# A Mamba-2 block in fp32: B times C and the state's output as one matmul group per row half of the TensorE array, on a PSUM ring of five banks

## The chip, the cores and the metric

One core of a Trainium2 chip runs the kernel. The metric is the device time of one execution in microseconds; less is better. All matrices are fp32. TensorE (PE in the profile) writes its products into PSUM, which has eight banks of 128 partitions by 2 KB; VectorE (DVE) and ScalarE (ACT) read them from there; GpSimd (POOL) works on SBUF alone; DMAs are issued from the queue of SyncE (SP).

## The reference

The block works on an input of 4 batches by 512 tokens by 512 channels. Six modulation vectors per batch come from a small matmul of `silu(c)`. Then:

```python
h = layernorm(x) * (1 + ca) + sa
x = x + ga * mamba2(h)                 # ga: at least 0.25 in size, sign kept
h = layernorm(x) * (1 + cb) + sb
x = x + gb * (h @ binarized(weight).T + bias)
```

and inside `mamba2`, with 64 heads of 16 channels, 8 groups of B and C with a state of 64, and chunks of 128 tokens:

```python
xBC, z, A = split(h @ in_proj_w.T)             # 2048, 1024 and 64 columns
xBC = silu(causal_conv_of_4_taps(xBC) + bias)  # then split into x, B, C
dt  = softplus(A);  dA = -dt
Lm  = exp(segsum(dA))                          # 128 x 128 decays for each head and chunk
Y_diag = (C B^T * Lm) X                        # within a chunk
Y_off  = C state * exp(cumsum(dA))             # from the chunks before
y   = (Y_diag + Y_off + D * x / dt) * silu(z + z_bias)
out = y @ out_proj_w.T
```

The state is carried from chunk to chunk of a batch (four chunks). `X` is the convolved x itself, as `x / dt * dt`.

## The kernel before

**Staging.** The 2048 tokens are cut into eight halves `h` of 256 tokens (two to a batch), each of two chunks `c` of 128 tokens. The 8 groups are taken in four pairs `gp`. A unit is `(h, c, gp)`, so there are 64 units, eight to a half. A unit has two groups, `r` = 0 and 1, which lie on partitions 0 to 63 and 64 to 127 of the tiles of B, C and the state; each has eight heads.

**Front of a half.** `f_norm` and `f_hT` make the normalized, transposed, modulated input. `f_dt` makes everything from `dt`: `pa` is the projection (L306); VectorE's softplus series follows (L309 to L322, one dependent step after another, with Abs and Exp on ACT at L310 and L311), ending in `ndt`; then `pe` (L330, L331) gives the decays to the chunk's end, `pc` (L344) the running sums, which go to DRAM (`sums_d`, `e_d`) to be read back broadcast over partitions; `pn` and `pr` (L353, L359) are transposes of small tiles. `f_B`, `f_C`, `f_x` are pairs of 128 columns of the input projection (L367 in `proj`) with the convolution: ACT's first tap at L379, VectorE's three taps at L383, tanh at L387, and the last product at L391. `f_C` writes C into `cd`, a tile with zeros in it: group `r` sits on its own 64 partitions and in its own 256 columns, block-diagonally, so that one matmul over all 128 partitions gives both groups. `f_Bt` and `f_xt` transpose B and x (`to_tokens`, L399). `f_z` projects the gate (L451 to L457).

**A unit** has three stages. `stage0` loads the running sums into two `decay` tiles and `e` by DMA. `stage1` multiplies B by C (`pg`, L509; 256 columns through `cd`), masks the result on VectorE (`gm`, L511), takes 16 exponentials on ACT (L516) and multiplies them by `gm` on VectorE (L519, twice). `stage2` forms the state's output (L543, again 256 columns through `cd`; not in a batch's first chunk) and 16 strip matmuls of 32 output columns each (L549), four of which lie side by side in the array; VectorE combines them (`yt`, L557 and L558), POOL finishes (L559, L562); then the new state's part `pst` (L574, two matmuls of 64 columns) is added by VectorE (L584, or copied at L577).

**Tail.** `tail1`, `tail2`, `tail3` do the output projection `po` (L606), the second norm, its transposes `ph` (L621) and the last projection `pf` (L634) for each chunk.

**Order.** The loop at the end calls these functions step by step from the table `FRONT`; step `s` works on unit `s` in `stage2`, on `s + 1` in `stage1` and on `s + 2` in `stage0`. The framework's scheduler then orders the instructions of each engine at build time by priority (the order of the calls) and by its own estimate of when they are ready, and adds the semaphores. Each engine takes its queue in that order. Tiles of one pool and tag share that tag's buffers in turn. PSUM accesses to one bank of one tile are kept in order, whichever part of it they touch.

**PSUM.** Four banks are a ring with the tag "mm" (projections, `po`, `ph`, `pf`), two are a ring "tr" (`pa`, `pe`, `pc`, `pn`, `pr`, `pt`, `pst`, `pm`), one holds `pg`, one `py`.

Of the kernel before, what the change touches and what calls it, by code (L numbers as in the profile page):

```python
# [1 line left out]

# [36 lines left out]
def adaln_mamba_block(  # L39
# [71 lines left out]

    cds = []
    for i in range(3):
        cd = keep.tile([P, 2, 2, T], F32, name=f"cd{i}")
        nc.gpsimd.memset(cd, 0.0)
        cds.append(cd)

    NE = 4
    decays = []
    for i in range(NE):  # L120
        et = keep.tile([P, HPG, CH], F32, name=f"decay{i}")
        nc.gpsimd.memset(et[CH // 2 :, :, 0 : CH // 2], 0.0)
        decays.append(et)


# [57 lines left out]
    def mod_cols(t6, slot):  # L183

        pg = mod_row(t6)
        row = wk.tile([B, DM], F32, tag="h2", name=f"row{t6}")
        nc.vector.tensor_scalar(row, pg, 1.0 if t6 in (1, 4) else 0.0, None, ALU.add)
        pm = ps.tile([P, NK, B], F32, tag="tr", bufs=2, name=f"pm{t6}")
# [15 lines left out]
    def gates_out():  # L204

        grow = wk.tile([B, 3, DM], F32, tag="gates", name="grow", bufs=1)
        brow = wk.tile([B, DM], F32, tag="th", name="brow", bufs=1)
# [88 lines left out]
    def f_dt(h):  # L296
# [5 lines left out]

        pa = ps.tile([P, W], F32, tag="tr", bufs=2, name=f"pa_{h}")
        for c in range(2):
# [23 lines left out]

        pe = ps.tile([P, 2, W], F32, tag="tr", bufs=2, name=f"pe_{h}")
        mm(pe[:, 0, :], after, ndt, start=True, stop=True)  # L330
# [10 lines left out]

        pc = ps.tile([NH, 2, 2, CH], F32, tag="tr", bufs=2, name=f"pc_{h}")
        for c in range(2):
# [6 lines left out]
        nc.sync.dma_start(e_d[h], es)  # L350
        pn = ps.tile([P, W], F32, tag="tr", bufs=2, name=f"pn_{h}")
        for c in range(2):
# [3 lines left out]

        pr = ps.tile([NH, 2, CH], F32, tag="tr", bufs=2, name=f"pr_{h}")
        for c in range(2):
# [10 lines left out]
    def conv_pair(h, t0, name, dst=None):  # L369

        u = wk.tile([P, 2, T], F32, tag="u", name=f"u_{name}_{h}", bufs=2)
# [11 lines left out]
        th = wk.tile([P, 2, T], F32, tag="th", name=f"th_{name}_{h}", bufs=1)  # L386
        nc.scalar.activation(th, u, AF.Tanh)  # L387
        if dst is None:
            dst = [(u, slice(0, P))]
        for d, r in dst:  # L390
            nc.vector.scalar_tensor_tensor(d, th[r], 1.0, u[r], ALU.add, ALU.mult)  # L391
        return u

    def to_tokens(src, name):

        pt = ps.tile([P, 2, 2, P], F32, tag="tr", bufs=2, name=f"pt_{name}")
        for c in range(2):
            for j in range(2):
                nc.tensor.transpose(pt[:, c, j, :], src[:, j, c * CH : (c + 1) * CH], ident)  # L399
        return pt  # L400

    def f_B(h, q):
        t = wk.tile([P, 2, T], F32, tag="B", name=f"B_{h}_{q}", bufs=3)
        conv_pair(h, DI // P + 2 * q, f"B{q}", [(t, slice(0, P))])
# [19 lines left out]
    def f_xt(h, j):  # L424
        xc = H[h].pop("xc")
        pt = to_tokens(xc, f"xt_{h}_{j}")
        xp = xpads[(4 * h + j) % NXP]
        nc.scalar.copy(
            xp.rearrange("p c (i q e) -> p (c i) q e", q=4, e=HD)[:, :, 0:4:3, :],
            pt.rearrange("p c j (i q e) -> p (c j i) q e", q=2, e=HD),  # L430
        )
        H[h]["xt"][j] = xp

        rr = wk.tile([P, 2, T], F32, tag="rr", name=f"rr_{h}_{j}", bufs=1)
        for r in range(2):
            lo = (2 * j + r) * HPG
            nc.sync.dma_start(
                rr[:, r, :],
                r_d[h, lo : lo + HPG].rearrange("h c s -> h (c s)").unsqueeze(1).to_broadcast([HPG, HD, T]),
            )  # L440
        xs = wk.tile([P, 2, T], F32, tag="xs", name=f"xs_{h}_{j}", bufs=4)
        nc.gpsimd.tensor_tensor(xs, xc, rr, ALU.mult)  # L442
        H[h]["xs"][j] = xs

    def f_z(h, j):
        pm = ps.tile([P, 2, T], F32, tag="mm", name=f"pp_z{j}_{h}")
        for q in range(2):
            proj(pm[:, q, :], h, NCONV + (2 * j + q) * P, KS - 1)
        u = wk.tile([P, 2, T], F32, tag="u", name=f"uz_{h}_{j}", bufs=2)
# [4 lines left out]
        th = wk.tile([P, 2, T], F32, tag="th", name=f"thz_{h}_{j}", bufs=1)  # L454
        nc.scalar.activation(th, u, AF.Tanh)
# [40 lines left out]

    def c_pair(h, c, gp):
        return H[h]["C"][gp // 2][:, gp % 2, :, c * CH : (c + 1) * CH]

    def stage1(h, c, gp):  # L500
# [6 lines left out]
        ets, e = U0.pop((h, c, gp))  # L507
        pg = ps.tile([P, 2, CH], F32, tag="g", name=f"pg_{n}", bufs=1)
        mm(pg, H[h]["B"][gp // 2][:, gp % 2, c * CH : (c + 1) * CH], c_pair(h, c, gp), start=True, stop=True)  # L509
        gm = wk.tile([P, 2, CH], F32, tag="gm", name=f"gm_{n}", bufs=3)  # L510
        nc.vector.tensor_mul(gm, pg, bc_mid(upto, 2))  # L511
        hd0 = c * NH + gp * HPP
# [11 lines left out]
    def stage2(h, c, gp):  # L524
# [15 lines left out]

        py = ps.tile([P, 2, 2, CH], F32, tag="y", name=f"py_{n}", bufs=1)
        if k > 0:
            mm(py[:, 1], states[b, k][:, gp, :], c_pair(h, c, gp), start=True, stop=True)  # L543

        for r in range(2):
            for q in range(2):
                for j in range(HPG // 2):
                    i = 2 * j + q
                    mm(py[32 * j : 32 * j + 32, 0, r, :], xp[:, r * 2 * P + 32 * i : r * 2 * P + 32 * i + 32],  # L549
                       ets[r][:, i, :], start=(q == 0), stop=(q == 1))  # L550

# [4 lines left out]
        if k > 0:  # L556
            nc.vector.tensor_mul(t, py[:, 1], e)  # L557
            nc.vector.tensor_add(t, py[:, 0], t)  # L558
            nc.gpsimd.tensor_add(t, t, xs)  # L559
        else:  # L560
            nc.vector.tensor_add(t, py[:, 0], xs)  # L561
        nc.gpsimd.tensor_mul(zg, t, zg)  # L562

        if k < HPB * 2 - 1:
# [111 lines left out]
    for step in range(-1, max(steps) + 1):  # L676
        ahead = step + 1 < len(units)

        late = step < 0 or step % NU == NU - 1
# [12 lines left out]

# [41 lines left out]
```

## Time and profile before

| | |
|---|---|
| median of three runs | 830.69 us (828.16 to 830.78) |
| profiled execution | 828.1 us; span from first to last instruction 826.4 us |
| granted TensorE clock, mean | 0.98 |
| busy: PE, weight loads, DVE, ACT, POOL | 773.7, 531.7, 647.4, 529.2, 258.2 us |
| DMA | 99.26 MB, mean 120 GB/s |

An fp32 matmul appears as two instructions of type MATMUL. In groups of instructions, a row gives the line, the engine, the operation, the tiles (written <- read), the shape, the count, busy time and mean nanoseconds of one, and idle time before it with what ended that. For PE, 128*32 is the part of the array in use, rows by columns; a matmul's shown duration includes its way through the array, so the distance between starts is what one costs in a stream. In the order of time, a row gives the start, the length, the engine and the group, and in brackets the idle time before it with its releaser. In the slices each digit is a tenth of busy time in a fortieth of the span.

### The profile page before, as it was taken

To read this page: it belongs to the slowest core of one execution; us is meant where nothing else is said; L and a number is where in the kernel's file an instruction comes from. 1 tells how busy PE (TensorE), PEld (TensorE's weight loads), DVE (VectorE), ACT (ScalarE), POOL (GpSimd) and SP (SyncE) were. 2 spreads that over 40 slices of the span, in tenths; PEclk is the share of its full clock that TensorE was granted. 3 is DMA by queue.
4 is the path that set the end of the run, shared out by engine and by line. 5 is a ranking of instruction groups with operands and counts; after the bars stand their busy time and mean duration, and the time that the engine had idled before them with its cause. 6 is when DMAs were issued, how large, how long until landed. Compare 5 with 4: busy or idle time off the path is not lost. (4 is left out here: it accounts for less than half of the span.)

```text
span 826.4 us, 14794 instructions
## 1 busy us (share of the span) xinstructions
PE 773.7 (94%) x5008; PEld 531.7 (64%) x5008; DVE 647.4 (78%) x1249; ACT 529.2 (64%) x1510; POOL 258.2 (31%) x293
## 2 busy tenths in 40 slices
PE   5979889999999999999999999999999999999875
PEld 0853657767667767667667767667667766667431
DVE  3688779995899669995899669996899768995742
ACT  0455485677667778577767678476758687676640
POOL 5020312353223412353223412253213521353431
PEclk9979999999999999999999999999999999999986
DMA  8856542525344372425444272344434382343620
GB/s 297 324 136 199 148 103 68 136 62 137 94 116 127 87 180 68 129 70 128 103 112 133 74 190 68 104 94 104 128 101 113 91 204 52 113 103 90 147 58 13
DMA packets 120139, 99.26 MB, mean 120 GB/s; under 512 B 73976, under 2 KB 98552, under 8 KB 120064
## 3 DMA queue, kind: packets, MB, share of 16 engines
q1 hardware_dynamic: 120064, 98.32, 44.9%
q8 instruction: 40, 0.66, 0.4%
q14 instruction: 35, 0.29, 0.1%
HBM read 92.50 MB, written 5.79 MB: 119 GB/s over the span
## 5 line engine op out<-in xcount | busy, mean ns | idle before, releaser
L516 ACT ACTIVATE decay<-decay,st 128x128 f32<-128x128 f32 x1024 | 313.8, 390 | 39.5 <-DMA decay<-sums_d 39.0
L519 DVE SCALAR_TENSOR_TENSOR decay<-decay,gm 128x1024 f32<-128x1024 f32 x128 | 168.4, 1322 | 11.4 <-ACT decay L516 10.6
L367 PE MATMUL pp_x<-hT,win 128*128 128x259 f32 x512 | 124.5, 393 | 3.4 <-DVE u_B L383 3.4
L606 PE MATMUL po<-wout,z 128*128 128x512 f32 x256 | 122.0, 615 | 5.3 <-POOL z L562 5.3
L367 PE MATMUL pp_z<-hT,win 128*128 128x256 f32 x512 | 115.1, 379 | 0.0
L367 PEld LDWEIGHTS pp_x<-hT,win 128*128 128x128 f32 x512 | 95.6, 193 | 23.0 <-issue 7.7
L367 PEld LDWEIGHTS pp_z<-hT,win 128*128 128x128 f32 x512 | 95.4, 189 | 15.7 <-issue 3.3
L549 PE MATMUL py<-decay,xpad 128*32 128x128 f32 x2048 | 81.8, 280 | 6.6 <-DVE decay L519 5.4
L383 DVE SCALAR_TENSOR_TENSOR u_x<-pp_x,cw,u_x 128x256 f32<-128x256 f32 x192 | 81.8, 476 | 2.2 <-ACT u_x L379 1.7
L442 POOL TENSOR_TENSOR xs<-u_x,rr 128x512 f32<-128x512 f32 x32 | 47.2, 1474 | 112.7 <-DVE u_x L391 68.1
L606 PEld LDWEIGHTS po<-wout,z 128*128 128x128 f32 x256 | 47.2, 194 | 51.6 <-issue 44.1
L549 PEld LDWEIGHTS py<-decay,xpad 128*32 128x32 f32 x2048 | 54.1, 111 | 36.0 <-issue 23.8
L569 POOL TENSOR_TENSOR xd<-xpad,ed 128x256 f32<-128x256 f32 x48 | 35.2, 732 | 131.4 <-PE pst L574 101.8
L562 POOL TENSOR_TENSOR z<-yt,z 128x256 f32<-128x256 f32 x64 | 66.7, 1042 | 30.4 <-DVE yt L561 18.9
L559 POOL TENSOR_TENSOR yt<-yt,xs 128x256 f32<-128x256 f32 x48 | 38.9, 811 | 111.1 <-DVE yt L558 110.9
L634 PE MATMUL pf<-bwT,h 128*128 128x512 f32 x128 | 63.5, 636 | 6.6 <-DVE u_x L383 5.8
L367 PE MATMUL pp_B<-hT,win 128*128 128x259 f32 x256 | 60.6, 382 | 0.0
L367 PE MATMUL pp_C<-hT,win 128*128 128x259 f32 x256 | 58.9, 381 | 0.0
L623 ACT ACTIVATE h<-ph,modT 128x128 f32<-128x128 f32 x64 | 24.5, 456 | 48.7 <-PE ph L621 48.7
L451 ACT ACTIVATE uz<-pp_z,zb 128x256 f32<-128x256 f32 x64 | 26.9, 466 | 43.7 <-PE pp_z L367 41.7
L367 PEld LDWEIGHTS pp_B<-hT,win 128*128 128x128 f32 x256 | 47.5, 190 | 11.2 <-issue 4.3
L367 PEld LDWEIGHTS pp_C<-hT,win 128*128 128x128 f32 x256 | 48.4, 190 | 7.4
(129 smaller groups left out, 1083.3 us busy)
## 6 DMA issues: line engine op xcount, KB each, us to landing
decay<-sums_d SPq DMA_DIRECT2D x128, 256.0 KB
decay<-sums_d SPq DMA_DIRECT2D x128, 128.0 KB
rr<-r_d SPq DMA_DIRECT2D x64, 128.0 KB
wm<-in_w_mod SPq DMA_DIRECT2D x24, 256.0 KB
e<-e_d SPq DMA_DIRECT2D x96, 64.0 KB
x<-in_x SPq DMA_DIRECT2D x16, 256.0 KB
win<-in_w_inT SPq DMA_DIRECT2D x4, 1024.0 KB
xr<-in_x SPq DMA_DIRECT2D x16, 256.0 KB
```

What stands on the lines that cost most here:

```text
L367: mm(pm, win[:, k, col : col + P], H[h]["hT"][:, k, lo:], start=(k == 0), stop=(k == NK - 1))
L383: nc.vector.scalar_tensor_tensor(u[:, j, :], pm[:, k : k + T], cw[:, t, k : k + 1], u[:, j, :], ALU.mult, ALU.add)
L442: nc.gpsimd.tensor_tensor(xs, xc, rr, ALU.mult)
L451: nc.scalar.activation(u[:, q, :], pm[:, q, :], AF.Identity, bias=zb[:, 2 * j + q : 2 * j + q + 1], scale=0.5)
L516: nc.scalar.activation(ets[r][:, i, :], ets[r][:, i, :], AF.Exp, bias=H[h]["st"][:, hd : hd + 1])
L519: nc.vector.scalar_tensor_tensor(ets[r], ets[r], 1.0, bc_mid(gm[:, r, :], HPG), ALU.min, ALU.mult)
L549: mm(py[32 * j : 32 * j + 32, 0, r, :], xp[:, r * 2 * P + 32 * i : r * 2 * P + 32 * i + 32], ets[r][:, i, :], start=(q == 0), stop=(q == 1))
L559: nc.gpsimd.tensor_add(t, t, xs)
L562: nc.gpsimd.tensor_mul(zg, t, zg)
L569: nc.gpsimd.tensor_tensor(xd, xg, by_head(H[h]["ed"][:, hd0 : hd0 + HPP]), ALU.mult)
L606: mm(po, H[h]["z"][g // 2][:, g % 2, c * CH : (c + 1) * CH], wout[:, g, :], start=(g == 0), stop=(g == NKI - 1))
L634: mm(pf, h2[:, k, :], bwT[:, k, :], start=(k == 0), stop=(k == NK - 1))
```

## The change

B times C and the state's output are no longer single matmuls against the block-diagonal `cd`. Each becomes two matmuls of 64 rows and 128 columns, one per row half of the array, whose results lie in two PSUM banks, one per row half (`gy`). `cd` and its zero fills are gone; `f_C` writes an ordinary tile with one VectorE instruction. The state's output of unit `s` and B times C of unit `s + 2` form one group, `glued`: its instructions are queued behind its first at a raised priority, ahead of the strips of unit `s`, which form a glued group of their own. `stage1` of unit `s + 2` now follows `stage0` of the same unit, for every step.

PSUM is laid out anew: the ring "mm" has five banks and takes over `pm`, `pe` and `pt`; `gy` holds two banks (slots 0 and 1 for the products, slots 2 and 3, as `pdt`, for `pa`, `pc`, `pn`, `pr` of `f_dt`); one bank, `pyst`, holds `py` and two slots of `pst` in turn. In SBUF `u` has three buffers instead of two, `th` and `rr` two instead of one. The number of lines grows: `pa` is at L309, `pe` at L333, `pf` at L650, the glued matmuls are at L496 (the first of a group) and L499 (the others).

```diff
-    ps = ctx.enter_context(tc.tile_pool(name="ps", bufs=4, space=PSUM))
+    ps = ctx.enter_context(tc.tile_pool(name="ps", bufs=5, space=PSUM))
...
-    cds = []
-    for i in range(3):
-        cd = keep.tile([P, 2, 2, T], F32, name=f"cd{i}")
-        nc.gpsimd.memset(cd, 0.0)
-        cds.append(cd)
...
+    bgy = ctx.enter_context(tc.tile_pool(name="bgy", bufs=1, space=PSUM))
+    gy = bgy.tile([P, 2, 4, CH], F32, name="gy")
+    pdt = gy[:, :, 2:4, :].rearrange("p b q s -> p b (q s)")
+
+    pyst = bgy.tile([P, 4, CH], F32, name="pyst")
...
-        pa = ps.tile([P, W], F32, tag="tr", bufs=2, name=f"pa_{h}")
+        pa = pdt[:, 0, 0:W]
...
-        pe = ps.tile([P, 2, W], F32, tag="tr", bufs=2, name=f"pe_{h}")
+        pe = ps.tile([P, 2, W], F32, tag="mm", name=f"pe_{h}")
...
-        pc = ps.tile([NH, 2, 2, CH], F32, tag="tr", bufs=2, name=f"pc_{h}")
+        pc = pdt[0:NH].rearrange("p c (q s) -> p c q s", q=2)
...
-        cd = cds[(2 * h + q) % 3]
-        conv_pair(
-            h, (DI + NG * NS) // P + 2 * q, f"C{q}",
-            [(cd[r * NS : (r + 1) * NS, :, r, :], slice(r * NS, (r + 1) * NS)) for r in range(2)],
-        )
-        H[h]["C"][q] = cd
+        t = wk.tile([P, 2, T], F32, tag="C", name=f"C_{h}_{q}", bufs=3)
+        conv_pair(h, (DI + NG * NS) // P + 2 * q, f"C{q}", t)
+        H[h]["C"][q] = t
...
+    def glued(products):
+        first = products[0]()
+        with tc.issue_after(first.ins), tc.high_priority(offset=1000):
+            for product in products[1:]:
+                product()
+
+    def by_rows(slot, h, c, gp, stationary):
+        return [
+            partial(
+                mm, gy[:, r, slot, :], stationary[part],
+                H[h]["C"][gp // 2][part, gp % 2, c * CH : (c + 1) * CH], start=True, stop=True,
+            )
+            for r, part in enumerate((slice(0, NS), slice(NS, P)))
+        ]
+
+    def state_out(h, c, gp):
+        k = (h % HPB) * 2 + c
+        return by_rows(1, h, c, gp, states[h // HPB, k][:, gp, :]) if k > 0 else []
+
+    def b_times_c(h, c, gp):
+        return by_rows(0, h, c, gp, H[h]["B"][gp // 2][:, gp % 2, c * CH : (c + 1) * CH])
...
-        pg = ps.tile([P, 2, CH], F32, tag="g", name=f"pg_{n}", bufs=1)
-        mm(pg, H[h]["B"][gp // 2][:, gp % 2, c * CH : (c + 1) * CH], c_pair(h, c, gp), start=True, stop=True)
...
-        py = ps.tile([P, 2, 2, CH], F32, tag="y", name=f"py_{n}", bufs=1)
-        if k > 0:
-            mm(py[:, 1], states[b, k][:, gp, :], c_pair(h, c, gp), start=True, stop=True)
+        py = pyst[:, 0:2, :]
...
-            pst = ps.tile([P, P], F32, tag="tr", bufs=2, name=f"pst_{n}")
+            pst = pyst[:, 2 + (c * NP + gp) % 2, :]
...
-        if ahead and not late:
-            stage1(*units[step + 1])
         for f, args in steps.get(step, []):
             f(*args)
-        if step < 0:
-            stage0(*units[0])
-        if 0 <= step < len(units):
-            stage2(*units[step])
-        if ahead and late:
-            stage1(*units[step + 1])
-        if step + 2 < len(units):
-            stage0(*units[step + 2])
+        new = units[step + 2 : step + 3] if step >= 0 else units[0:2]
+        if step < 0:
+            for unit in new:
+                glued(b_times_c(*unit))
+                stage0(*unit)
+                stage1(*unit)
+        elif step < len(units):
+            products = state_out(*units[step])
+            for unit in new:
+                products += b_times_c(*unit)
+            if products:
+                glued(products)
+            stage2(*units[step])
+            for unit in new:
+                stage0(*unit)
+                stage1(*unit)
```

More of the change, by code (lines that the diff above doesn't have):

```diff
@@ L1 @@
 from contextlib import ExitStack
+from functools import partial
 import numpy as np
@@ L187, in mod_cols @@
         nc.vector.tensor_scalar(row, pg, 1.0 if t6 in (1, 4) else 0.0, None, ALU.add)
-        pm = ps.tile([P, NK, B], F32, tag="tr", bufs=2, name=f"pm{t6}")
+        pm = ps.tile([P, NK, B], F32, tag="mm", name=f"pm{t6}")
         for dt in range(NK):
@@ L206, in gates_out @@
         grow = wk.tile([B, 3, DM], F32, tag="gates", name="grow", bufs=1)
-        brow = wk.tile([B, DM], F32, tag="th", name="brow", bufs=1)
+        brow = wk.tile([B, DM], F32, tag="th", name="brow")
         nc.sync.dma_start(brow, ffn_b.partition_broadcast(B))
@@ L350, in f_dt @@
         nc.sync.dma_start(e_d[h], es)
-        pn = ps.tile([P, W], F32, tag="tr", bufs=2, name=f"pn_{h}")
+        pn = pdt[:, 0, 0:W]
         for c in range(2):
@@ L355, in f_dt @@
         nc.vector.tensor_scalar(st, pn, -1.0, None, ALU.mult)
-        pr = ps.tile([NH, 2, CH], F32, tag="tr", bufs=2, name=f"pr_{h}")
+        pr = pdt[0:NH, 1, :].rearrange("p (c s) -> p c s", c=2)
         for c in range(2):
@@ L369, in conv_pair @@
     def conv_pair(h, t0, name, dst=None):
-        u = wk.tile([P, 2, T], F32, tag="u", name=f"u_{name}_{h}", bufs=2)
+        u = wk.tile([P, 2, T], F32, tag="u", name=f"u_{name}_{h}", bufs=3)
         for j in range(2):
@@ L385, in conv_pair @@
                 )
-        th = wk.tile([P, 2, T], F32, tag="th", name=f"th_{name}_{h}", bufs=1)
+        th = wk.tile([P, 2, T], F32, tag="th", name=f"th_{name}_{h}")
         nc.scalar.activation(th, u, AF.Tanh)
[L388 to L391, printed above, removed]
+        nc.vector.scalar_tensor_tensor(u if dst is None else dst, th, 1.0, u, ALU.add, ALU.mult)
         return u
     def to_tokens(src, name):
-        pt = ps.tile([P, 2, 2, P], F32, tag="tr", bufs=2, name=f"pt_{name}")
+        pt = ps.tile([P, 2, 2, P], F32, tag="mm", name=f"pt_{name}")
         for c in range(2):
@@ L403, in f_B @@
         t = wk.tile([P, 2, T], F32, tag="B", name=f"B_{h}_{q}", bufs=3)
-        conv_pair(h, DI // P + 2 * q, f"B{q}", [(t, slice(0, P))])
+        conv_pair(h, DI // P + 2 * q, f"B{q}", t)
         H[h]["B"][q] = t
     def f_C(h, q):
-        cd = cds[(2 * h + q) % 3]
-        conv_pair(
-            h, (DI + NG * NS) // P + 2 * q, f"C{q}",
-            [(cd[r * NS : (r + 1) * NS, :, r, :], slice(r * NS, (r + 1) * NS)) for r in range(2)],
-        )
-        H[h]["C"][q] = cd
+        t = wk.tile([P, 2, T], F32, tag="C", name=f"C_{h}_{q}", bufs=3)
+        conv_pair(h, (DI + NG * NS) // P + 2 * q, f"C{q}", t)
+        H[h]["C"][q] = t
     def f_Bt(h, q):
@@ L432, in f_xt @@
         H[h]["xt"][j] = xp
-        rr = wk.tile([P, 2, T], F32, tag="rr", name=f"rr_{h}_{j}", bufs=1)
+        rr = wk.tile([P, 2, T], F32, tag="rr", name=f"rr_{h}_{j}")
         for r in range(2):
@@ L448, in f_z @@
             proj(pm[:, q, :], h, NCONV + (2 * j + q) * P, KS - 1)
-        u = wk.tile([P, 2, T], F32, tag="u", name=f"uz_{h}_{j}", bufs=2)
+        u = wk.tile([P, 2, T], F32, tag="u", name=f"uz_{h}_{j}", bufs=3)
         for q in range(2):
@@ L453, in f_z @@
             )
-        th = wk.tile([P, 2, T], F32, tag="th", name=f"thz_{h}_{j}", bufs=1)
+        th = wk.tile([P, 2, T], F32, tag="th", name=f"thz_{h}_{j}")
         nc.scalar.activation(th, u, AF.Tanh)
@@ L495, in stage0 @@
         U0[h, c, gp] = (ets, e)
-    def c_pair(h, c, gp):
-        return H[h]["C"][gp // 2][:, gp % 2, :, c * CH : (c + 1) * CH]
+    def glued(products):
[16 more added lines that the diff above has]
+        return by_rows(0, h, c, gp, H[h]["B"][gp // 2][:, gp % 2, c * CH : (c + 1) * CH])
     def stage1(h, c, gp):
@@ L507, in stage1 @@
         ets, e = U0.pop((h, c, gp))
-        pg = ps.tile([P, 2, CH], F32, tag="g", name=f"pg_{n}", bufs=1)
-        mm(pg, H[h]["B"][gp // 2][:, gp % 2, c * CH : (c + 1) * CH], c_pair(h, c, gp), start=True, stop=True)
         gm = wk.tile([P, 2, CH], F32, tag="gm", name=f"gm_{n}", bufs=3)
-        nc.vector.tensor_mul(gm, pg, bc_mid(upto, 2))
+        nc.vector.tensor_mul(gm, gy[:, :, 0, :], bc_mid(upto, 2))
         hd0 = c * NH + gp * HPP
@@ L539, in by_head @@
             return v.rearrange("p (j q) -> p j q", q=2).unsqueeze(3).to_broadcast([P, HPG, 2, HD])
-        py = ps.tile([P, 2, 2, CH], F32, tag="y", name=f"py_{n}", bufs=1)
-        if k > 0:
[L543 to L550, printed above, removed]
+        py = pyst[:, 0:2, :]
+        glued([
+            partial(
+                mm, py[32 * j : 32 * j + 32, r, :],
+                xp[:, r * 2 * P + 32 * (2 * j + q) : r * 2 * P + 32 * (2 * j + q) + 32],
+                ets[r][:, 2 * j + q, :], start=(q == 0), stop=(q == 1),
+            )
+            for r in range(2) for q in range(2) for j in range(HPG // 2)
+        ])
         cs = slice(c * CH, (c + 1) * CH)
@@ L556, in stage2 @@
         if k > 0:
-            nc.vector.tensor_mul(t, py[:, 1], e)
-            nc.vector.tensor_add(t, py[:, 0], t)
+            nc.vector.tensor_mul(t, gy[:, :, 1, :], e)
+            nc.vector.tensor_add(t, py, t)
             nc.gpsimd.tensor_add(t, t, xs)
         else:
-            nc.vector.tensor_add(t, py[:, 0], xs)
+            nc.vector.tensor_add(t, py, xs)
         nc.gpsimd.tensor_mul(zg, t, zg)
@@ L676, in adaln_mamba_block @@
     for step in range(-1, max(steps) + 1):
-        ahead = step + 1 < len(units)
-        late = step < 0 or step % NU == NU - 1
-        if ahead and not late:
-            stage1(*units[step + 1])
         for f, args in steps.get(step, []):
             f(*args)
+        new = units[step + 2 : step + 3] if step >= 0 else units[0:2]
         if step < 0:
-            stage0(*units[0])
-        if 0 <= step < len(units):
+            for unit in new:
[8 more added lines that the diff above has]
+                glued(products)
             stage2(*units[step])
-        if ahead and late:
-            stage1(*units[step + 1])
-        if step + 2 < len(units):
-            stage0(*units[step + 2])
+            for unit in new:
+                stage0(*unit)
+                stage1(*unit)
 _OUT = ((B, L, DM), np.float32)
```

## The prediction

> **What bounds the kernel now.** I read the page's totals and slices first, then the stretches, then the order of time around the spots that the change touches.
>
> ```profile
> PE 773.7 (94%) x5008; PEld 531.7 (64%) x5008; DVE 647.4 (78%) x1249; ACT 529.2 (64%) x1510; POOL 258.2 (31%) x293
> PE   5979889999999999999999999999999999999875
> DVE  3688779995899669995899669996899768995742
> PEclk9979999999999999999999999999999999999986
> ```
> TensorE is busy nearly all the time between the ramp and the tail, at full clock. The view of stretches says it sharper: of the 100 us from 125 to 225, PE is busy for 99.45, DVE for 83.81, ACT for 67.79. So in the middle a microsecond of TensorE work, or of TensorE waiting, is a microsecond of the kernel.
>
> The order of time on TensorE, once around a half's `f_dt` (from `pa` to `pe`):
>
> ```profile
> 301.33 1.22 PE L306 MATMUL pa<-win,hT 128*128 128x64 f32 x10
> 302.39 5.37 PE L606 MATMUL po<-wout,z 128*128 128x512 f32 x12
> 307.60 3.67 PE L367 MATMUL pp_B<-hT,win 128*128 128x259 f32 x16
> 311.11 3.67 PE L367 MATMUL pp_C<-hT,win 128*128 128x259 f32 x16
> 314.61 0.59 PE L543 MATMUL py<-cd,S 128*128 128x256 f32 x2
> 315.13 1.08 PE L549 MATMUL py<-decay,xpad 128*32 128x128 f32 x32
> 316.14 0.70 PE L509 MATMUL pg<-cd,B 128*128 128x256 f32 x2
> 316.68 0.60 PE L621 MATMUL ph<-ident,t 128*128 128x128 f32 x4
> 318.49 0.49 PE L330 MATMUL pe<-ndt,after 128*128 128x128 f32 x2 [1.20 <-DVE ndt L322]
> ```
> `pe` needs `ndt`, the end of VectorE's softplus chain (L309 to L322) that starts from `pa`. Today 16 us of output and input projections stand between the two in TensorE's queue, and still `pe` waits 1.20 us. Over the eight halves the waits for `ndt` come to 3.9 us. The chain itself, from groups by line and, for its spacing, VectorE's order of time:
>
> ```profile
> L318 DVE SCALAR_TENSOR_TENSOR da<-da,dq 128x128 f32<-128x128 f32 x56 | 18.7, 333 | 0.1
> L313 DVE RECIPROCAL dr<-dr 128x128 f32<-128x128 f32 x8 | 7.6, 952 | 0.2
> ```
> ```profile
> 401.05 0.29 DVE L314 TENSOR_TENSOR ds<-du,dr 128x128 f32<-128x128 f32 x1
> 401.38 0.29 DVE L315 TENSOR_TENSOR dq<-ds 128x128 f32<-128x128 f32 x1
> ```
> A dependent step of 0.29 us is followed 0.33 us later: 0.04 us per hop.
>
> The prices of the matmuls that change, from TensorE's order of time:
>
> ```profile
> 425.57 0.59 PE L543 MATMUL py<-cd,S 128*128 128x256 f32 x2
> 426.09 1.08 PE L549 MATMUL py<-decay,xpad 128*32 128x128 f32 x32
> 427.10 0.70 PE L509 MATMUL pg<-cd,B 128*128 128x256 f32 x2
> 427.64 3.60 PE L634 MATMUL pf<-bwT,h 128*128 128x512 f32 x8
> ```
> Starts tell more than durations. `pp_B` above takes 3.51 us for 16 instructions of 259 columns (307.60 to 311.11), so a column costs 0.85 ns and an instruction of 256 columns about 0.21 us. The state's output (two instructions, 0.43) runs from 425.57 to 426.09, 0.52: changing the array's shape to 128x32 strips costs 0.09. B times C after the strips takes 0.54: 0.11 of weight load stands uncovered there. The 32 strips take 1.01; at 0.107 each in one line they would take 3.4, so four column groups do run side by side.
>
> **The change, part by part.**
>
> Columns streamed. `pg` (64 units) and the state's output (48 units) each stream 256 columns, half of them against zeros: 112 x 0.427 = 47.8 us. Afterwards each is two products of 64 rows and 128 columns, in separate row halves. If the halves run together, 112 x 0.213 = 23.9 us: **-23.9**. No row of this trace has two row halves at once. Bounds: no overlap (0) and full overlap (-23.9). I take full, by the nearest rows, the column groups (strips, 3.4 us of work in 1.01).
> The Trainium skill ("TensorE: Matmul & The Clock Gate", Part 3, the table of measured packings) gives 3.07x for four row tiles; two would then gain about 1.5x (an estimate from that page). By it this term would be -16 us and the total some 8 us higher.
>
> Shape switches. In the programs' orders of issue the array changes shape 307 times before and 352 times after, since the glued row-half group seldom stands next to the strips. Price of an entry: 0.09 for any switch, plus the uncovered load, 0.11 for 128 columns, 0.025 for strips: 0.2 into full or row-half shape, 0.12 into strips. Entries into strips fall from 103 to 71 (-3.8), into the full shape rise from 128 to 137 (+1.8), into row halves from 8 to 76 (+13.6): **+11.6**.
>
> The new wait. `pe` now comes from the ring "mm", ahead of the projections in program order, and `pa`, `pc`, `pn`, `pr` lie in gy's banks, so products of later units stand behind the whole `f_dt`. In the order of issue of the changed program `pe` follows the last `pa` with nothing between in five halves; in halves 3, 5 and 7 only a `pst` and 16 strip matmuls are between (1.6 us by the rows above). TensorE issues in order, so `pc`, `po`, `pp_B`, `pp_C` all queue behind `pe`, and ACT and VectorE wait for those.
> The bare chain: `dl` 0.29, Abs 0.28, Exp 0.31, 0.22, reciprocal 0.95, two of 0.29, 0.22, seven of 0.33, two of 0.28, `ndt` 0.48, together 6.2; 16 hops at 0.04 make 6.8; the end of the last `pa` matmul 0.27: **7.1 us**. That is what halves 0 and 1 lose.
> In halves 2, 4 and 6 the order puts eight decay exponentials (2.44 us in the trace) between Abs and Exp on ACT, and two L519 products (1.3 each) inside VectorE's chain: 7.1 + 2.4 + 2.6, less 0.4 for the first product's start beside Exp, 11.7.
> In halves 3, 5, 7 the exponentials come after Exp; two L519 and one S copy (0.28) are inside, less what ACT's 0.6 covers: 9.4, of which 1.6 is worked: 7.8.
> Sum 2 x 7.1 + 3 x 11.7 + 3 x 7.8 = 72.7; less today's 3.9: **+68.8**. Bounds: 6.2 each, less the worked 4.8 and 3.9, +40.9; and +80 if the exponentials wait for their loads as well.
>
> The clock. After long idle the granted clock is halved for a while. The chain of waits at the end has it, after 3.85 us of idle:
>
> ```profile
> 815.74 6.22 PE pf L634 x8
> ```
> Those are the same eight instructions that took 3.60 above: 2.6 lost. The milder row, `pf` at 520.18, took 4.51 for six (2.7 at full clock): 1.8 lost. Eight waits at 2.2: **+17.6** (14 to 21; nothing if the clock stays).
>
> New waits on banks. `py` and `pst` now share the bank pyst, so strips wait for the copy or sum of the last state (0.28 plus crossings) and `pst` for `yt` (0.42). In the order of issue strips follow a `pst` directly 10 times, a `pst` follows a row-half group after strips 12 times: 22 x 0.5 = 11 at most, against middle stalls of today (`pf` 1.95 us at 520.18 and its like, about 10) that idle time elsewhere lets VectorE catch up on. I take 0, bounds -10 and +20.
>
> At no cost: `cd`'s two VectorE writes (29.0 us) become one (about 13), and three POOL memsets of 0.95 go; both engines have slack, so no gain either. The moved `stage1` of a half's first unit (16 exponentials, two L519, no DMA) comes one unit earlier, beside projections; if uncovered it is 2.6 us in eight places, and it is partly priced in the chain already. `stage0`'s loads keep their place on SP's queue except at the start, where unit 1's four go ahead of the half's later `rr` loads, behind the weight loads that hold that queue anyway. More buffers for `u`, `th`, `rr` only remove waits.
>
> **Sum.** 826.4 - 23.9 + 11.6 + 68.8 + 17.6 = 900.5 us span. The profiled execution took 828.1, 1.7 more than its span: 902. (It is 2.6 below the median of the runs shown, 830.69; I do not correct for that.)
>
> **Rivals.**
> Faster: the idle time at `pe` is won back, because VectorE, at 9 in most slices, sets the pace of the convolution stretches. Then only the matmul terms stay: 826.4 - 23.9 + 11.6 + 1.7 = 816. It decides from the point where the unrecovered wait is under 1.5 us per half (12.3 / 8). Against it: PE 99.45 of 100 us beside DVE 83.81. 4%.
> Row halves do not overlap: 902 + 23.9 = 926. No row excludes it; the strips speak against it. 15%.
> A lighter wait: only the bare chain in every half (8 x 7.1 - 4.8 - 3.9 = 48.1) and no clock lost: 864. For it: ACT may be ahead and have the exponentials done. Against it: both slow-clock rows. 18%.
> My forecast, 902: 62%. The last 1% is no change.
>
> **How the numbers follow.** About 0.3% is what a measurement of this kernel can tell from no change. Faster 0.04, same 0.01, slower 0.95. The range goes from just under the lighter case (with its bank term at -8: 856) to just over the no-overlap case: 930.
>
> **What would show it.** Right: TensorE's idle before `pe` (now L333) of some 70 us in eight places of 7 to 12; eight dips of the granted clock; `gy` groups whose four products start within about 0.4 us; VectorE's L321 back to back. Wrong: `pe` waits of a few us in all, or a DVE busy share near 99% between them.

## The result and the profile after

The changed kernel takes 966.48 us (median of four runs, 965.72 to 969.02) against 830.74 us for the kernel before: 1.165 times as long, 95% interval 1.1616 to 1.1679. The forecast had the sign and half of the size: 902, with a range up to 930.

The page of the changed kernel, its totals and three of its slices:

```profile
PE 802.8 (83%) x5232; PEld 543.1 (56%) x5232; DVE 642.6 (67%) x1233; ACT 534.1 (55%) x1510; POOL 253.5 (26%) x290
PE   5777868889589988889599897889689897899975
DVE  2578746785578836885668935886568944885661
PEclk9798978999799997999799997999889997999987
```

No engine is full. VectorE and GpSimd are busy for less time than before (642.6 us against 647.4, 253.5 against 258.2), ScalarE for 4.9 us more; TensorE's 802.8 against 773.7 contains the matmuls that ran at half clock. TensorE's 94% of 826.4 us have become 83% of 964.4, and the granted clock, 0.980 on average before, is 0.909. The holes come in a period of two halves.

The waits of TensorE (line waited for, total, times, longest):

```profile
PE pe L333 <- DVE ndt L325: 44.7, 5, 10.5
PE pyst L496 <- DVE decay L535: 18.3, 7, 4.6
PE gy L496 <- DVE gm L527: 14.4, 9, 3.0
PE pyst L499 <- DVE decay L535: 13.5, 8, 2.8
PE po L622 <- POOL z L578: 10.0, 5, 3.9
...
PE pt_bt L399 <- DVE B L391: 8.7, 11, 1.3
```

The first row is the wait that was forecast. In TensorE's order of time it looks like this in half 2, and in half 3 it lies in front of the strips that the order has put between `pa` and `pe`:

```profile
244.94 1.78 PE L309 MATMUL gy<-win,hT 128*128 128x64 f32 x14
257.25 0.80 PE L333 MATMUL pe<-ndt,after 128*128 128x128 f32 x2 [10.53 <-DVE ndt L325]
...
363.28 0.42 PE L496 MATMUL pyst<-decay,xpad 128*32 128x128 f32 x1 [4.61 <-DVE decay L535]
...
366.57 1.08 PE L499 MATMUL pyst<-decay,xpad 128*32 128x128 f32 x16 [2.21 <-DVE decay L535]
...
367.58 0.80 PE L333 MATMUL pe<-ndt,after 128*128 128x128 f32 x2
```

After 10 us of idleness `pe` itself takes 0.80 us for what took 0.49 before: half clock. VectorE's and ScalarE's order of time in that hole:

```profile
247.08 0.28 ACT L313 ACTIVATE du<-gy 128x128 f32<-128x128 f32 x1 [1.97 <-DVE dl L312]
247.26 2.43 ACT L532 ACTIVATE decay<-decay,st 128x128 f32<-128x128 f32 x8
249.59 0.30 ACT L314 ACTIVATE du<-du 128x128 f32<-128x128 f32 x1
249.72 1.23 DVE L535 SCALAR_TENSOR_TENSOR decay<-decay,gm 128x1024 f32<-128x1024 f32 x1 [2.67 <-ACT decay L532]
...
252.90 1.22 DVE L535 SCALAR_TENSOR_TENSOR decay<-decay,gm 128x1024 f32<-128x1024 f32 x1
254.04 2.24 DVE L321 SCALAR_TENSOR_TENSOR da<-da,dq 128x128 f32<-128x128 f32 x7
```

The eight exponentials between Abs and Exp and the two products inside the chain are where the order of issue had them.

What was not forecast is the other holes. A matmul that needs nothing new stands behind one that does:

```profile
312.32 0.63 PE L399 MATMUL pt_bt<-ident,B 128*128 128x128 f32 x4 [1.25 <-DVE B L391]
312.79 3.67 PE L370 MATMUL pp_x<-hT,win 128*128 128x259 f32 x16
```

`pp_x` needs only `hT`, which had been complete since 245 us. And the units come bunched. The view of stretches (busy time of each engine, in us, and number of instructions), for half 3's approach:

```profile
316.00:326.80 10.80, 8.85 (x71) 6.44 (x70) 9.77 (x21) 9.20 (x30) 5.24 (x5) 0.84 0.50 119
326.80:352.00 25.20, 25.20 (x100) 17.33 (x98) 12.19 (x21) 11.12 (x29) 5.33 (x6) 1.00 0.07 23
352.00:368.80 16.80, 9.69 (x138) 7.29 (x138) 10.75 (x26) 10.42 (x31) 3.49 (x7) 0.79 0.61 156
```

Columns after the stretch and its length: PE, PEld, DVE, ACT, POOL, clock, DMA share, GB/s. For 25 us TensorE does hardly anything but projections, and VectorE, the third engine of the row, is busy for 12.19; then the units' small matmuls come all together (138 in 16.8 us), and TensorE is busy for 9.69. The 7.1 us that it idles there are, but for 0.3, the forecast wait of half 3 shown above (4.61 and 2.21), so these rows show the bunching and not a new wait. The waits that were not forecast are short and scattered: from 240 to 470 us, two halves, TensorE's waits come to 31.6 us, of which 10.53 and 6.82 are the forecast ones and the other 14 lie in 18 places, the longest of them 2.6 us. In the kernel before, the like stretch gives VectorE steady work:

```profile
333.00:358.00 25.00, 24.39 (x168) 18.20 (x168) 24.42 (x53) 17.47 (x46) 10.21 (x12) 1.00 0.43 109
```

**The account of the difference.** From the starts of all matmuls in both traces: the distance from one start to the next, less 0.833 ns per column (divided by the tiles that run side by side), is split by kind; gaps over 0.35 us count as waits, and the extra of a matmul while the records show half clock counts as clock. A wait at a change of the array's shape leaves about 0.13 us, what a change costs without a wait, to the switches. The columns do not depend on such choices; other ways of dividing move the last three rows by some 4 us against each other.

| us | before | after | difference | forecast |
|---|---|---|---|---|
| columns streamed | 677.6 | 653.7 | -23.9 | -23.9 |
| shape switches | 41.5 | 49.9 | +8.4 | +11.6 |
| half clock | 10.0 | 37.4 | +27.4 | +17.6 |
| waits | 43.2 | 158.9 | +115.7 | +68.8 and 0 for banks |
| small gaps | 39.6 | 51.5 | +11.9 | 0 |

That is +139.5 from the first matmul's start to the last one's; the span grew by 138.0.

### The profile page after: what moved, and what is told of

It is laid out like the page before. It is cut to its first block, busy times and chain, and to the rows that moved or that the text cites. A ratio compares the mean times of both kernels' runs of the same rounds, so it can differ in the third digit from the quotient of the medians.

```text
span 964.4 us, 15124 instructions
## 1 busy us (share of the span) xinstructions
PE 802.8 (83%) x5232; PEld 543.1 (56%) x5232; DVE 642.6 (67%) x1233; ACT 534.1 (55%) x1510; POOL 253.5 (26%) x290
## 4 chain that ended last, share of the span: by engine, by line
PE 53%; DVE 19%; issue 13%; ACT 6%; DMA 4%; POOL 3%; SPq 1%; ACTq 0%; DVEq 0%; POOLq 0%
PE pp_z L370 11%; PE pp_x L370 9%; PE po L622 8%; PE pf L650 6%; DVE decay L535 4%; DVE u_x L386 3%; ACT decay L532 3%; PE pyst L499 3%; PE pp_B L370 2%; PE pt_xt L399 2%; PE pg L183 2%; DMA decay<-sums_d 2%; DVE u_B L386 2%; PE pp_C L370 2%; PE gy L309 1%
## 5 line engine op out<-in xcount | busy, mean ns | idle before, releaser
L622 PE MATMUL po<-wout,z 128*128 128x512 f32 x256 | 128.9, 637 | 10.0 <-POOL z L578 10.0
L370 PE MATMUL pp_x<-hT,win 128*128 128x259 f32 x512 | 131.6, 411 | 0.0
L370 PEld LDWEIGHTS pp_x<-hT,win 128*128 128x128 f32 x512 | 103.3, 208 | 17.8 <-issue 1.3
L386 DVE SCALAR_TENSOR_TENSOR u_x<-pp_x,cw,u_x 128x256 f32<-128x256 f32 x192 | 87.9, 478 | 19.9 <-ACT u_x L382 17.9
L499 PE MATMUL pyst<-decay,xpad 128*32 128x128 f32 x1920 | 79.1, 294 | 13.5 <-DVE decay L535 13.5
L578 POOL TENSOR_TENSOR z<-yt,z 128x256 f32<-128x256 f32 x64 | 61.7, 964 | 47.4 <-DVE z L454 25.5
L499 PEld LDWEIGHTS pyst<-decay,xpad 128*32 128x32 f32 x1920 | 54.7, 116 | 20.0 <-DVE decay L535 16.7
L650 PE MATMUL pf<-bwT,h 128*128 128x512 f32 x128 | 64.0, 639 | 0.6 <-ACT h L639 0.6
L454 DVE SCALAR_TENSOR_TENSOR z<-thz,uz 128x512 f32<-128x512 f32 x32 | 28.5, 891 | 49.2 <-ACT thz L452 48.8
L382 ACT ACTIVATE u_x<-pp_x,cb,cw 128x256 f32<-128x256 f32 x64 | 36.0, 562 | 36.1 <-PE pp_x L370 35.9
L370 PEld LDWEIGHTS pp_B<-hT,win 128*128 128x128 f32 x256 | 48.0, 191 | 10.8 <-issue 4.1
L382 ACT ACTIVATE u_B<-pp_B,cb,cw 128x256 f32<-128x256 f32 x32 | 17.9, 561 | 64.5 <-PE pp_B L370 64.3
```

The costliest lines, as they stand in the source:

```text
L370: mm(pm, win[:, k, col : col + P], H[h]["hT"][:, k, lo:], start=(k == 0), stop=(k == NK - 1))
L382: nc.scalar.activation(u[:, j, :], pm[:, KS - 1 :], AF.Identity, bias=cb[:, t : t + 1], scale=cw[:, t, KS - 1 : KS])
L386: nc.vector.scalar_tensor_tensor(u[:, j, :], pm[:, k : k + T], cw[:, t, k : k + 1], u[:, j, :], ALU.mult, ALU.add)
L454: nc.vector.scalar_tensor_tensor(z, th, 1.0, u, ALU.add, ALU.mult)
L499: product()
L622: mm(po, H[h]["z"][g // 2][:, g % 2, c * CH : (c + 1) * CH], wout[:, g, :], start=(g == 0), stop=(g == NKI - 1))
```

## The experiments

Theory A: `pe` stands in the ring "mm" ahead of the projections, TensorE waits for `ndt`, and that is most of the loss. Rivals: the other new sharing (f_dt in gy, `py` with `pst`) loses time by itself; the other waits follow from the first; and, once the first results were there, theory G: `pt` has the same fault as `pe`. Where no interval is given, a run is a single time beside a run of the kernel before at 830.45 to 830.99.

**pe alone, in the kernel before (e1).**

```diff
-        pe = ps.tile([P, 2, W], F32, tag="tr", bufs=2, name=f"pe_{h}")
+        pe = ps.tile([P, 2, W], F32, tag="mm", name=f"pe_{h}")
```

> The kernel before, with one edit: pe comes from the ring mm, as in the changed kernel. In the order of issue pe then stands 3 to 6 us of unit work (strips, pg, py) after the last pa, and the projections stand behind it; in the first half it stands directly after pa. Theory A (pe's place in the ring is what makes TensorE wait for the softplus chain): the wait for ndt rises from 3.9 us to between 25 and 45 us and brings half-clock windows of 10 us or more, so 860 to 880 us. Theory B (the ring does not matter; the waits of the changed kernel come from its other sharing of PSUM): 828 to 836 us, wait for ndt under 8 us.

913.42 us: 83 us for one word. But the wait is hardly at `pe`. The waits of this run:

```profile
PE py L549 <- DVE decay L519: 40.7, 24, 3.8
PE py L543 <- DVE yt L558: 12.3, 11, 2.6
PE pt_bt L399 <- DVE B L391: 9.9, 8, 2.1
...
PE pe L330 <- DVE ndt L322: 6.5, 1, 6.5
```

The scheduler fills the place before `pe` with the strips and products of the units, no projection passes it, and the strips wait for decays in its stead: between the last `pa` and `pe` TensorE idles for 57 us in the eight halves, 6.2 to 8.3 in each. This is theory A's mechanism at a larger cost than expected (860 to 880); the row of the trace that bears `pe`'s name shows 6.5 us of it. Who looks for a misplaced tile must look at what stands ahead of it, too.

**pe, f_dt and pst out of the way, in the changed kernel (e2, e3, e4).** e2 puts `pe` into the f_dt slots of gy:

```diff
-        pe = ps.tile([P, 2, W], F32, tag="mm", name=f"pe_{h}")
+        pe = pdt[:, 1, :].rearrange("p (q w) -> p q w", q=2)
```

e3 gives `pa`, `pe`, `pc`, `pn`, `pr` a bank of their own (`tag="dt", bufs=1`) with four banks in "mm"; e4 is e2 with `pst` in a bank of its own, again with four.

> The changed kernel with pe moved out of the ring mm into the f_dt slots of gy; the ring keeps its five banks. In the order of issue output and input projections stand between pa and pe again. Theory A (the wait for the chain and its half clock, some 65 + 20 us, are a loss by themselves, and the other 50 us of new waits stand on their own): 875 to 890 us. Theory B (the other waits are a consequence too, engines thrown out of step by the stalls): 815 to 840 us. Theory C (the wait only moves, since the products of later units stand behind f_dt in gy): 940 us or more.

> The changed kernel with all of f_dt (pa, pe, pc, pn, pr) in a bank of its own and the ring mm at four banks; gy holds products alone. Theory A (pe's wait alone, other waits stand on their own): as with pe in gy, 875 to 890 us. Theory D (f_dt in gy holds up the products of the units for the length of the chain and starves VectorE and ScalarE): 15 us or more below the run with pe in gy, 835 to 865 us.

> The changed kernel with pe in the f_dt slots of gy, pst in a bank of its own and the ring mm at four banks. Theory E (py and pst in one bank make pst wait for yt, 12 us in the trace, and strips wait for the copy or sum of the state, and these waits are a loss by themselves): 12 to 20 us below the run with pe in gy and five banks. Theory F (those instructions would wait for decays or xd anyhow): within 5 us of it, or above it if the fifth bank of the ring is worth something.

934.53, 907.70 and 910.73 us. None meets its numbers. `pe` out of the ring brings 32 us, not 80; freeing gy or separating `pst`, each with a bank fewer in the ring, brings 27 and 24 more, as theories D and E had it in direction; and all three stay 77 us or more above the kernel before. No run changes the fifth bank of the ring alone, so it stays open how much of the 27 and 24 comes from it. In e2 the largest wait had become that of `pt_xt` (21.3 us, for `u_x`), in e3 that of `pt_bt` (16.4 us, for B). That led to theory G.

**pt alone (e8), and pt and f_dt out of the ring (e5).** In the kernel before, e8 moves only `pt` into the ring; e5 is e3 with `pt` in the same bank of its own (`tag="tr", bufs=1` for all of them). The edit of e8:

```diff
-        pt = ps.tile([P, 2, 2, P], F32, tag="tr", bufs=2, name=f"pt_{name}")
+        pt = ps.tile([P, 2, 2, P], F32, tag="mm", name=f"pt_{name}")
```

> The kernel before with only pt moved into the ring mm, pe left in tr. Theory G (pt in the projections' ring costs by itself): 850 to 890 us, with waits for B and u_x at pt and for decays at the strips. Theory H (only pe's place matters): 828 to 836 us.

> The changed kernel with all of f_dt and pt too taken out of the ring mm and of gy, into one bank of their own; mm has four banks. With f_dt alone moved, 32 us of waits for B and u_x before pt were left. Theory G (pt has the same fault as pe: a tile that gets ready late stands in the ring ahead of the projections, units bunch up before it and are missing later): 815 to 845 us. Theory H (the waits at pt are a consequence of VectorE being late through the shared banks gy and pyst): 885 us or more.

e8: 926.14 us, 95 more than before. e5: 816.94 us, 0.983 of the kernel before (0.9794 to 0.9871), 91 less than e3. Theory G holds both ways, though e8 lies above its 850 to 890, and theory H, lateness through shared banks, falls: e3 and e5 differ in `pt` alone, and in e5 the two products still share gy, and `py` and `pst` a bank. TensorE's order of time in e8 shows the two steps:

```profile
251.73 0.66 PE L399 MATMUL pt_bt<-ident,B 128*128 128x128 f32 x4 [1.88 <-DVE B L391]
252.22 0.60 PE L621 MATMUL ph<-ident,t 128*128 128x128 f32 x4
252.66 3.67 PE L367 MATMUL pp_x<-hT,win 128*128 128x259 f32 x16
256.17 0.59 PE L543 MATMUL py<-cd,S 128*128 128x256 f32 x2
256.69 1.08 PE L549 MATMUL py<-decay,xpad 128*32 128x128 f32 x32
...
260.05 1.15 PE L549 MATMUL py<-decay,xpad 128*32 128x128 f32 x32
263.79 0.94 PE L543 MATMUL py<-cd,S 128*128 128x256 f32 x2 [2.59 <-DVE yt L558]
264.52 1.06 PE L399 MATMUL pt_xt<-ident,u_x 128*128 128x128 f32 x4
265.37 4.71 PE L367 MATMUL pp_x<-hT,win 128*128 128x259 f32 x16
```

First TensorE waits at `pt_bt` with projections behind it. Then, with no projection ahead of `pt_xt`, the scheduler puts two units in a row before it; the first product of a third waits 2.59 us for VectorE to be done with the second, and the clock falls (4.71 us for what takes 3.67).

**pe alone, in the repaired kernel (e11).** e5 with `pe` back in "mm":

> The kernel with f_dt and pt in a bank of their own (817 us), with pe alone put back into the ring mm. Here products and strips of the units may stand between pa and pe, which the changed kernel does not allow. If pe in the ring costs by itself what it costs in the kernel before (83 us): 880 to 910 us. If the units between cover the chain: 817 to 835 us.

899.16 us, 82 more than e5; between the last `pa` and `pe` TensorE idles for 52 us in the eight halves. So in either kernel `pe` alone costs some 82 and `pt` alone 91 to 95. Both together cost less than the sum (the changed kernel, with `f_dt` in gy as well, is 150 us above e5), presumably because the same projections can be held up only once. The 902 of the forecast is near the time of this kernel, in which `pe` alone of the two is in the ring.

**Only the order of calls (e9), and both (e10).** e9 keeps every bank and ring of the changed kernel:

```diff
+    def f_dt2(h):          # from the allocation of pe to the end of f_dt
...
-        (4, f_B, (0,)), (4, f_C, (0,)), (4, f_Bt, (0,)),
-        (5, f_x, (0,)), (5, f_xt, (0,)), (5, f_x, (1,)), (6, f_xt, (1,)),
-        (6, f_B, (1,)), (6, f_C, (1,)), (6, f_Bt, (1,)),
-        (7, f_x, (2,)), (7, f_xt, (2,)), (7, f_x, (3,)), (8, f_xt, (3,)), (8, f_z, (0,)),
+        (4, f_B, (0,)), (4, f_C, (0,)), (4, f_dt2, ()),
+        (5, f_x, (0,)), (5, f_Bt, (0,)), (5, f_x, (1,)), (6, f_xt, (0,)),
+        (6, f_B, (1,)), (6, f_xt, (1,)), (6, f_C, (1,)),
+        (7, f_x, (2,)), (7, f_Bt, (1,)), (7, f_x, (3,)), (8, f_xt, (2,)), (8, f_z, (0,)), (8, f_xt, (3,)),
```

> The changed kernel with every bank and ring as changed (five banks in mm, pe and pt in it, the rest of f_dt in gy, py and pst in one bank); only the order of calls differs: f_dt is cut behind ndt and drdt and its second part is called after f_C of the first pair; f_Bt and f_xt are called one projection later. Theory G (a tile that gets ready late holds up what was called after it in its ring; which banks there are matters little): 810 to 835 us. Theory I (the sharing of gy and pyst, and the ring's load of late tiles, cost by themselves): 880 us or more.

> The kernel with f_dt and pt in a bank of their own (817 us) and, on top, the new order of calls. If what is left of waits for ndt, B and u_x (9.5 us in its trace) goes with the later calls: 806 to 814 us. If the later calls make the units' inputs late: 820 us or more.

e9: 840.24 us, 1.0106 of the kernel before (1.007 to 1.0142), 5 us above theory G's range and 40 below theory I's. The order of calls alone takes back 126 of the 136 us, with not one tile in another bank. This is the direct test: in these traces the front's tiles of one ring get their first writes in the order of the calls. TensorE's order in half 2, shortened, then the first writes of the front's tiles over one half:

```
changed: pa (strips) pa  pe  pc  po  ...                     everything behind pe
e9:      po pa (strips) po (products) po pp_B pp_C (strips)  pe  pc  ph  pp_x ...

changed: pe pp_B pp_C pt_bt pp_x pt_xt pp_x pt_xt pp_B pp_C pt_bt ...     as called
before:  pp_B pp_C pe pp_x pt_bt pp_x pt_xt pp_B pt_xt pp_C pp_x pt_bt ... pe, pt in the ring tr
e9:      pp_B pp_C pe pp_x pt_bt pp_x pt_xt pp_B pt_xt pp_C pp_x pt_bt ... as called
```

In the kernel before, whose calls are in the old order, the scheduler lets each `pt` come a projection later than it is called; e9's calls make almost the same order by hand.

e10 adds the new order to e5: 811.63 us, 0.9777 of the kernel before (0.9748 to 0.9806), the fastest kernel of this study. e9 is 28.6 us above it: there `pe` and `pt` are still in the ring, `f_dt` is in gy, and the ring has five banks. `py` and `pst` share a bank in both. The waits of e9:

```profile
PE pe L337 <- DVE ndt L325: 16.9, 8, 4.6
...
PE po L626 <- POOL z L582: 9.5, 6, 4.0
PE pyst L594 <- DVE yt L581: 6.1, 4, 3.0
...
PE pt_xt L403 <- DVE u_x L395: 5.7, 8, 1.3
```

In e10 the first of these is 6.1 us and the second 7.9, and the last two do not appear: 24 us of waits less. How much of the 28.6 goes to the tiles that are still late, to gy and to the fifth bank was not taken apart.

**The matmul part (e6, e7, e12, e13, e14).** e7 is the kernel before with one bank instead of two in "tr"; e6 is e7 with row halves:

```diff
-        mm(pg, H[h]["B"][gp // 2][:, gp % 2, c * CH : (c + 1) * CH], c_pair(h, c, gp), start=True, stop=True)
+        by_rows(0, h, c, gp, H[h]["B"][gp // 2][:, gp % 2, c * CH : (c + 1) * CH])
...
+    def by_rows(slot, h, c, gp, stationary):
+        for r in range(2):
+            part = slice(r * NS, (r + 1) * NS)
+            mm(gy[:, r, slot, :], stationary[part], c_pair(h, c, gp)[part, r, :], start=True, stop=True)
```

> The kernel before with its ring tr cut from two banks to one, nothing else: the control of the run with row halves alone. 828 to 836 us if the second bank is not needed; if pt, pst and f_dt hold each other up in one bank, 840 us or more.

> The kernel before with only the two products per row half: B times C and the state's output go to two banks gy (slots 0 and 1) as two products of 64 rows and 128 columns each, the strips have a bank of their own, the ring tr is cut to one bank to make room; order of calls, no glue and the ring mm as before. If the term of -23.9 us for the columns and +8 to +12 for the shape switches are right and the bank shared by the two products costs nothing: 812 to 822 us. If sharing gy between B times C and the state's output is itself a loss: 835 us or more.

e7: 830.06, so the second bank of "tr" was not needed. e6: 830.82 us, ratio 1.000 (0.9979 to 1.0021). The row halves alone gain nothing, and not for want of overlap: in e6's starts the columns are down by the full 23.9 us, but switches are up by 16.8 and small gaps by 7.2. In the order of calls of before, B times C and the state's output stand apart, and each pays its own entry into the row halves.

e12 is e10 with block-diagonal C and whole-array products, and the buffers of `u`, `th`, `rr` as before to make room; e13 is e10 with those buffers alone; e14 is e10 without the raised priority in `glued`.

> The fastest kernel so far (812 us) with its two products back on the whole array: block-diagonal C, one matmul of 256 columns each, B times C in one bank and the state's output in the other; u, th and rr have the buffers of the kernel before, to make room for the zeros. Compared with its control, the same buffers with row halves. By the prediction's terms (-23.9 us of columns, +11.6 of shape switches): 10 to 14 us slower than the control. By the run of the kernel before with row halves alone, which gained nothing: within 3 us of it.

> The control: the fastest kernel so far with u, th and rr at two, one and one buffers, as in the kernel before. If these buffers only hide waits that are hidden anyway: 809 to 815 us. If they carry part of the gain: 818 us or more.

> The fastest kernel so far with the products and strips issued as plain matmuls, without the raised priority that keeps a group together. In the order of issue the array changes shape 27 times more, at 0.1 to 0.2 us each: 814 to 818 us if that is the glue's worth; 811 to 813 us if the scheduler keeps the groups together well enough; 820 us or more if the order of the rest changes too.

825.71 us (ratio 0.9934, 0.9909 to 0.996), 818.09 (0.9856, 0.983 to 0.9882) and 816.91 (0.9839, 0.981 to 0.9868). Row halves in a group are worth 7.6 us, between the two expectations; by the starts of the two profiled executions, which lie 8.9 us apart, 23.9 us of columns less 10.8 us of switches, and some 4 us lost again, more to half clock and small gaps than is won in waits. The glue is worth 5.3 us, as expected from 27 switches, the extra buffers 6.5; what waits for these buffers stays open.

## Why the prediction was wrong

**The columns: right.** -23.9, and the row halves do overlap, the step without a row in the trace of before. TensorE's order of time around one group of the changed kernel:

```profile
300.55 0.37 PE L496 MATMUL gy<-C,S 64*128 64x128 f32 x1
300.56 0.37 PE L499 MATMUL gy<-C,S 64*128 64x128 f32 x1
300.76 0.27 PE L496 MATMUL gy<-C,S 64*128 64x128 f32 x1
300.77 0.27 PE L499 MATMUL gy<-C,S 64*128 64x128 f32 x1
300.87 0.39 PE L499 MATMUL gy<-C,B 64*128 64x128 f32 x4
301.19 0.30 PE L496 MATMUL pyst<-decay,xpad 128*32 128x128 f32 x1
```

The two halves start 0.01 us apart, and the whole group, eight instructions, takes 0.64 us to the first strip (301.19 less 300.55), where the two products took 0.52 and 0.54 each by themselves. The Trainium skill ("TensorE: Matmul & The Clock Gate", Part 3) had led to an estimate of 1.5 times for two row tiles; the runs show 2 for the streaming, so the row of the strips was the better guide.

**Shape switches: right in size.** +11.6 forecast, +8.4 in the changed kernel, 10.8 between e12 and e13. e6, with 16.8, shows what holds it down: the pair as one group.

**The new wait at pe: right, place by place.** From the last `pa` to `pe` the trace has 6.8, 7.0, 10.8, 9.6, 10.8, 9.6, 10.8 and 9.6 us in the eight halves; the forecast worked out 7.1, 7.1, 11.7, 9.4 (7.8 and 1.6 of strips), and so on. As waits these are 44.7 at `pe` and three times 4.61 + 2.21 at the strips before it, 65.2 in all, 61.3 more than the 3.9 of before, for +68.8. In e1 and e11, where `pa` is not in gy and more unit work stands ahead of `pe`, the waits stand before that work instead, 57 and 52 us between `pa` and `pe`: the work between did not cover the chain. One row was misread beside it, without effect on the sum: of the 16 us between `pa` and `pe` in the kernel before, 12.2 are projections (302.39 to 314.61) and the rest is unit work, a transpose and the wait.

**New waits on banks: the step that failed.** It was put at 0 with a bound of +20. Beside the 61.3 the trace has some 54 us of other new waits (115.7 less 61.3), and the clock and gaps that exceed the forecast (9.8 and 11.9 us) presumably came with them. The bound was made from the banks that `py` and `pst`, or two products, share. The tile that mattered is in the diff's account of the change, "takes over `pm`, `pe` and `pt`", and the prediction followed `pe` alone. The reason it gave for `pe`, a tile that is ready late and stands in the ring ahead of projections, holds for `pt` as well, whose inputs B and `u_x` end a convolution on VectorE: e8 puts it at 95 us alone, e3 against e5 at 91. The forecast priced `pt`'s move at nothing and gave no reason. What the rest of the change adds to a kernel with `pe` in the ring is 67 us (966.48 less e11's 899.16), and the forecast missed by 64. A half has six `pt` tiles (two `pt_bt`, four `pt_xt`) against one `pe`; in the changed kernel they cost little at their own line (8.7 us at `pt_bt`, 4.0 at `pt_xt`), and the larger part shows elsewhere, in units that come bunched.

**The clock: right for the eight dips, too small in all.** 17.6 forecast for eight dips; the trace records 178 us at half clock in 30 stretches, against 34.9 us in 6, and 27.4 us more are lost. The eight dips at `pe` are there. The forecast tied a dip to a long wait; most of the others come with bunched units and waits of 0.3 to 3 us, as the last section shows.

**The rivals.** "Faster" (816) needed the waits to be won back. They were not. Its case was also put too strongly: VectorE's slices of before show a 9 in 17 of 40, not in most. But its number is close to that of the kernel without them, e5 at 816.94, whose starts have the columns down by 23.9 us, the switches up by 6.7 and the waits up by only 3.9. "No overlap" and "a lighter wait" are both refuted by the rows above. The rival that was missing is a second tile with the same fault.

## What to carry to other kernels

When tiles change their ring, list every tile that joins it, with the work that must end before its first write, and ask of each what was called after it in that ring; in these runs a late tile held all of that up, and the scheduler filled the place with work that then waited itself. The order of calls is the cheapest repair: calling the users of the late tiles one or two projections later took back 126 us without touching a bank. Price an array packing by the switches into it as well as by its columns: the same row halves were worth nothing apart and 8 us as a group.

## What the runs showed of the hardware

Two row halves of the array, writing two PSUM banks, run fully side by side in fp32: starts 0.01 us apart, and 0.11 us per pair of 128-column instructions in a stream. The half-clock stretches in the clock records of the changed kernel are 3.4, 6.8, 10.2 or 13.7 us long, but for the last, and idle stretches of 2 to 3 us between short matmuls come before them too, as in the rows of e8 above, where 2.59 us of waiting came just before `pp_x` at 4.71. What decides is not one wait's length. In the kernel before, the same wait of 1.95 us stands before `pf` at 333.61, 520.18 and 708.79, and only the second is followed by half clock (4.51 us for what takes 2.81). On the grid of 3.41 us on which the records change, the window before each change tells more: in the changed kernel 29 windows at full clock are followed by half clock, and in 27 of these TensorE is busy for at most 50% by the profile's busy time (68 and 86% in the other two), while in the 197 that are followed by full clock it is busy for 52% or more; in the kernel before, at most 43% in 5 and 49% or more in 222. The Trainium skill ("TensorE: Matmul & The Clock Gate", Part 1) gives a window of about 3.4 us for the gate; the lengths of the stretches agree with it.
